# A linear attention's product of keys and values: whole 128x128 blocks against each head's own 32x32 block in four column groups

## The chip, the cores and the metric

The kernel runs on one core of a Trainium2 chip. The metric is the device time of one execution in microseconds (us). The core has a matrix engine (TensorE, PE in the profile, with its weight loads shown apart as PEld), VectorE (DVE), ScalarE (ACT), GpSimd (POOL) and a queue for transfers (SyncE, SP). Each engine works through its own list of instructions in order and waits on semaphores for the others.

## The reference

Two layers, each an attention and a feed-forward part with a layer norm after each. The change touches the attention of the first layer, a linear attention with 16 heads of 32 columns over 2 sequences of 1024 rows of 512 columns:

```
q = _feature_map(proj(Wq))          # elu(y) + 1, heads of 32 columns
k = _feature_map(proj(Wk))
v = proj(Wv)
kv = jnp.einsum('bhtd,bhte->bhde', k, v)
z = 1.0 / (jnp.einsum('bhtd,bhd->bht', q, k.sum(axis=2)) + 1e-06)
out = jnp.einsum('bhtd,bhde,bht->bhte', q, kv, z)
out = out.transpose(0, 2, 1, 3).reshape(b, t, c)
return jnp.einsum('btc,oc->bto', out, Wo)
```

`kv` is one 32x32 block for each head. All inputs are fp32.

## The kernel before

**Tiling.** The 2048 rows are four blocks of 512 (`blk`), two for each sequence (`b`). P is 128 and KC is 4, the number of 128-column tiles in 512 columns. `c` counts such a tile and `j` a head within it, so that column c*128 + 32*j begins one head.

**The order of products.** v is never formed. `add_xk` (L441) sums G = x^T k over a sequence in four PSUM banks (512x512) and copies it to `G_of[b]`. `values` (L501) then multiplies Wv with G. Of that 512x512 product only the 32x32 block of each head is needed. Before the change each 128x128 block on the diagonal is formed, one for each c: four matmuls over k, 128 columns of weights, 128 columns streamed, into one bank `vk` (L508). Each such block holds its four heads' blocks on its own diagonal and twelve others that nobody reads. ScalarE copies the whole bank to `vkm` (L512). `G_rows` (L530) multiplies each head's block with the 32 rows of Wo of that head: sixteen 32x32 matmuls of 512 columns (L538), tile `gp`, in four banks, head j of all tiles in bank `gp[j]`; ScalarE copies them back to `G_of[b]` (L542). The output is q times this G (`o_products`, L560, line L572), added to x.

**What stands around it.** `q_products(j)` is a product by seven multiplications (`by_seven`, L385), given as a generator that yields between its steps; its matmuls are at L396, tiles `grow`, `P2` and `P7` (both shown as `P`). `run` (L660) puts other work between its steps. For the second block j of a sequence the steps are these: the first product (`grow`), then `values(b)`; the second product (`P2`; its sum into the pair is L414 on VectorE), then `turned(i, 0)` and `turned(i, 1)`, two transposes of 128 rows of q of the block before (L239 called from L552, tile `qTp`, copied out by ScalarE at L558); two more products, then `turned(i, 2)`, `turned(i, 3)`, `q_sums` (L521) and `G_rows(b)`; then the products of the output.

The rows that `turned` transposes have been scaled on VectorE by `weigh` (L484): for each 128 rows a product with the sums of k (L491), a sum over each head (L492), an addition (L493), a reciprocal (L494) and a multiplication (L496). In the second sequence, `L414` is queued behind the last of these by hand (`behind_add`), and so is the split of x's transposes (L273). ScalarE's exponentials in `elu1` (L345) are L350 and L351, VectorE's part L352. VectorE also unpacks the feed-forward weights in this time (L293, L294).

**What sets the order.** The matmuls follow each other in the order in which the code is written: `behind()` (L367) ties each group to the last one (`last_pe`). On the other engines a few instructions are tied by `tc.issue_after`; the order of the rest is sorted when the program is built.

**Banks.** `mm_bank` takes two banks by turns, so that vk has the bank that P7 of the product before had (read by L432), P2 of its own product has the other, and P7 of its own product takes vk's bank again. `acc_bank` takes four by turns: the four `qTp`, then the four `gp` in the same banks. So `gp[j]` waits for the copy L558 of `turned(i, j)`.

## Time and profile before

| | us |
|---|---|
| median of 3 runs | 873.0 (872.01 to 873.72) |
| the profiled execution, its own time | 872.3 |
| its span in the profile | 870.5 |
| PE busy | 861.3 (99%), 4067 matmul passes |
| PE weight loads busy | 682.9 (78%) |
| DVE busy | 681.4 (78%) |
| ACT busy | 373.7 (43%) |
| POOL busy | 265.0 (30%) |
| vk, passes (L508) | 64 of 0.275 each, first at 72.7, last at 186.6 |
| vkm, copy (L512) | 2 of 0.586 |
| gp, passes (L538) | 64 of 0.600 each, first at 83.3, last at 195.4 |

The span is what the profile's records cover; the time holds 1.8 us more around it. The 16 matmuls of vk in each batch show as 32 passes, since each fp32 matmul is recorded as two. A pass's duration reaches from its start to its modelled end, and passes overlap, so that what a row of passes costs is read from their starts. Times of single instructions below are from the start of the span; a line of a timeline gives start, length, engine, code line, operation, output<-inputs and shape, and in brackets the idle time ahead of it and what ended that.

### The profile page before, as it was taken

The page shows a single profiled execution, that of the slowest core. Times are in us where ns is not written, and L with a number is a line of the kernel's source. Part 1 is how long each engine was busy: PE and PEld are TensorE (multiplying, and loading weights), DVE is VectorE, ACT ScalarE, POOL GpSimd, SP SyncE. Part 2 cuts the span into 40 slices and gives each one's busy share as a digit, 9 for nine tenths or more (in the row PEclk, how much of TensorE's full clock was granted, in tenths as well). Part 3 has the DMA queues.
Part 4 walks back from the last instruction along what each step waited for, and adds up shares of the span by engine and source line. Part 5 has one row for each costly group of instructions (what it writes and reads, how often), then busy time and mean ns, then how long its engine had stood idle before and what let it go on. Part 6 is the DMA issues. An engine that isn't in the chain of part 4 may idle for free.

```text
span 870.5 us, 11281 instructions
## 1 busy us (share of the span) xinstructions
PE 861.3 (99%) x4067; PEld 682.9 (78%) x4067; DVE 681.4 (78%) x1340; ACT 373.7 (43%) x636; POOL 265.0 (30%) x249
## 2 busy tenths in 40 slices
PE   9999999999999999999999999999999999999996
PEld 6667886678578888888887787888686888888885
DVE  3668984988877788887787988677988988998525
ACT  2345333453468797787886624132210222210000
POOL 2120020830474367457556312030520210000112
PEclk9999999999999999999999999999999999999999
DMA  9632212210241302504301654000154140320001
GB/s 336 225 104 66 82 50 78 73 49 12 68 152 49 49 1 55 91 1 120 75 0 37 133 99 193 1 1 1 38 117 161 50 74 28 118 97 1 25 24 49
DMA packets 103848, 64.87 MB, mean 75 GB/s; under 512 B 80078, under 2 KB 80634, under 8 KB 103281
## 3 DMA queue, kind: packets, MB, share of 16 engines
q1 hardware_dynamic: 101153, 58.89, 24.0%
q0 software_dynamic: 1920, 4.22, 1.3%
q10 hardware_dynamic: 720, 1.05, 0.4%
q8 instruction: 32, 0.52, 0.3%
q14 instruction: 23, 0.19, 0.1%
HBM read 48.37 MB, written 17.88 MB: 76 GB/s over the span
## 4 chain that ended last, share of the span: by engine, by line
PE 88%; issue 4%; POOL 3%; DVE 3%; DMA 1%; POOLq 0%; ACT 0%; DVEq 0%
PE hp L1696 11%; PE yp L1790 11%; PE go L921 10%; PE yp L953 9%; PE gatep L953 9%; PE upp L953 9%; PE grow L396 4%; PE xk L448 4%; PE P L396 3%; PE ao L1561 3%; PE grow L572 2%; POOL x L223 2%; PE kp L646 2%; PE P L572 2%; PE grow L1521 2%
## 5 line engine op out<-in xcount | busy, mean ns | idle before, releaser
L1018 DVE TENSOR_TENSOR yp<-yp,ratio 128x512 f32<-128x512 f32 x160 | 103.2, 693 | 18.2 <-PE yp L953 16.2
L978 ACT ACTIVATE gatep<-gatep,scale 128x512 f32<-128x512 f32 x132 | 84.0, 659 | 36.3 <-PE gatep L953 33.3
L218 POOL TENSOR_TENSOR rs<-rs,table 128x4 f32<-128x4 f32 (+1 forms) x19 | 16.6, 875 | 251.2 <-DVE rs L217 250.9
L953 PE MATMUL yp<-wdn,hhi 128*128 128x512 f32 x176 | 70.3, 399 | 0.2 <-DVE yp L1018 0.2
L953 PE MATMUL gatep<-x1Th,wgu 128*128 128x512 f32 x176 | 70.3, 400 | 0.0
L953 PE MATMUL yp<-wdn,hlo 128*128 128x512 f32 x176 | 69.9, 397 | 0.2 <-POOL hlo L987 0.2
L953 PE MATMUL gatep<-x1Tl,wgu 128*128 128x512 f32 x176 | 69.1, 393 | 0.0
L953 PE MATMUL upp<-x1Tl,wgu 128*128 128x512 f32 x176 | 68.9, 391 | 0.0
L953 PE MATMUL upp<-x1Th,wgu 128*128 128x512 f32 x176 | 68.9, 391 | 0.0
L978 ACT ACTIVATE upp<-upp,scale 128x512 f32<-128x512 f32 x100 | 64.8, 663 | 6.6 <-PE upp L953 3.1
L987 POOL TENSOR_TENSOR hlo<-whole,hhi 128x512 fp32r<-128x512 f32 x43 | 55.5, 1291 | 3.5
L986 POOL CAST hhi<-whole 128x512 fp32r<-128x512 f32 x43 | 26.3, 611 | 86.4 <-DVE whole L984 85.7
L984 DVE SCALAR_TENSOR_TENSOR whole<-upp,scale,silu 128x512 f32<-128x512 f32 x43 | 32.3, 750 | 19.8 <-PE upp L953 12.2
L921 PE MATMUL go<-spare,spare 128*128 128x256 f32 x192 | 44.1, 382 | 0.0
L448 PE MATMUL xk<-pair,x 128*128 128x512 f32 x96 | 42.7, 592 | 0.0
L230 DVE BATCH_NORM_STATS2 st<-x 128x6 f32<-128x512 f32 x64 | 42.3, 676 | 0.3
L953 PEld LDWEIGHTS yp<-wdn,hhi 128*128 128x128 f32 x176 | 33.1, 188 | 10.3 <-DVE yp L1018 1.3
L953 PEld LDWEIGHTS gatep<-x1Th,wgu 128*128 128x128 f32 x176 | 33.1, 188 | 9.1 <-ACT gatep L978 1.1
L921 PEld LDWEIGHTS go<-spare,spare 128*128 128x128 f32 x192 | 36.1, 190 | 5.1
L953 PEld LDWEIGHTS yp<-wdn,hlo 128*128 128x128 f32 x176 | 33.1, 188 | 7.8 <-POOL hlo L987 0.6
L953 PEld LDWEIGHTS gatep<-x1Tl,wgu 128*128 128x128 f32 x176 | 33.1, 188 | 7.5 <-issue 0.2
L953 PEld LDWEIGHTS upp<-x1Th,wgu 128*128 128x128 f32 x176 | 33.1, 188 | 7.3 <-DVE rw L984 0.2
(461 smaller groups left out, 2036.2 us busy)
## 6 DMA issues: line engine op xcount, KB each, us to landing
pk<-in_gu SPq DMA_DIRECT2D x16, 352.0 KB, 3.6
x<-in_x SPq DMA_DIRECT2D x4, 1024.0 KB, 14.1
w<-in_w SPq DMA_DIRECT2D x1, 4096.0 KB, 12.6
w<-in_w SPq DMA_DIRECT2D x4, 1024.0 KB, 5.3
out<-x SPq DMA_DIRECT2D x4, 1024.0 KB, 4.2
x0T<-in_xT SPq DMA_DIRECT2D x3, 1024.0 KB, 7.3
x1r<-x SPq DMA_DIRECT2D x3, 1024.0 KB, 4.3
x1S<-x1r SPq DMA_DIRECT2D x12, 256.0 KB, 4.5
```

The source lines that it names most:

```text
L230: nc.vector.bn_stats(st, x)
L396: ins = nc.tensor.matmul(ps[:, 256 * r : 256 * r + 256], a[:, k, r * P : (r + 1) * P], b[:, k], start=first and r == 0 and k == 0, stop=k ...
L448: ins = nc.tensor.matmul(acc_of[b][c], x_t[blk][:, i, c * P : (c + 1) * P], pairs_of["k", blk][i // 2][:, i % 2], start=blk % 2 == 0 and i ...
L572: ins = nc.tensor.matmul(ps[:, 256 * r : 256 * r + 256], a[:, k, r * P : (r + 1) * P], b[:, k], start=first and r == 0 and k == 0, stop=k ...
L921: ins = nc.tensor.matmul(ps[:, 256 * m : 256 * m + 256], w[:, k, m], b[:, k, 256 * half : 256 * half + 256], start=first and m == 0 and k ...
L953: nc.tensor.matmul(ps, w, x, start=start and n == 0, stop=stop and n == 1, skip_group_check=True)
L978: nc.scalar.activation(ps, ps, AF.Copy, scale=s)
L984: nc.vector.scalar_tensor_tensor(self.whole, ps, s, self.silu, ALU.mult, ALU.mult)
L987: nc.gpsimd.tensor_sub(lo, self.whole, hi.bitcast(F32))
L1018: nc.vector.tensor_tensor(self.y[:, i] if g == NI - 1 else ps, ps, ratio[:, g], ALU.mult)
L1696: ins = nc.tensor.matmul(ps[:, 256 * j : 256 * j + 256], pair_of(w, g)[:, k, j], x[:, k], start=k == 0, stop=k == 1).ins
L1790: nc.tensor.matmul(ps[:, 256 * r : 256 * r + 256], x(r, j), w(j), start=j == 0, stop=j == NJ - 1)
```

## The change

In `values`, each head's block is formed alone. A matmul takes the head's 32 columns of Wv as weights and streams the head's 32 columns of G, both over 128 rows. Head j's result goes to partitions 32*j to 32*j + 31 of the bank, that is to the j-th group of 32 of the array's columns, and to columns 32*c to 32*c + 31. The four heads of a tile follow each other inside the loop over k. There are 64 matmuls per batch where there were 16. `vkm` has 32 columns for each tile instead of 128, ScalarE copies 128 columns of the bank instead of 512, and `G_rows` takes its weights from the narrower tile.

```diff
         with behind():
             for c in range(KC):
-                cut = slice(c * P, (c + 1) * P)
                 for k in range(KC):
-                    ins = nc.tensor.matmul(vk[:, cut], Wv[:, k, cut], G_of[b][:, k, cut], start=k == 0, stop=k == KC - 1).ins
+                    for j in range(4):
+                        head = slice(c * P + 32 * j, c * P + 32 * j + 32)
+                        ins = nc.tensor.matmul(
+                            vk[32 * j : 32 * j + 32, 32 * c : 32 * c + 32], Wv[:, k, head], G_of[b][:, k, head],
+                            start=k == 0, stop=k == KC - 1, skip_group_check=True,
+                        ).ins
         last_pe[0] = ins
-        vkm_of[b] = wk.tile([P, KC, P], F32, tag="vkm", name="vkm", bufs=1)
-
-        nc.scalar.copy(vkm_of[b], vk.rearrange("p (c d) -> p c d", c=KC))
+        vkm_of[b] = wk.tile([P, KC, 32], F32, tag="vkm", name="vkm", bufs=1)
+
+        nc.scalar.copy(vkm_of[b], vk[:, :P].rearrange("p (c d) -> p c d", c=KC))
...
-                        gp[j][quad(c)], vkm_of[b][quad(j), c, quad(j)], Wo[quad(j), c], start=True, stop=True
+                        gp[j][quad(c)], vkm_of[b][quad(j), c], Wo[quad(j), c], start=True, stop=True
```

## The prediction, made before the changed kernel was run

> **What bounds the kernel now.** I read the busy shares in 40 slices first, then the busy time by stages, then the chain of waits, then the timelines around the two places that the change touches.

> ```profile
> PE   9999999999999999999999999999999999999996
> ...
> DVE  3668984988877788887787988677988988998525
> ```

> ```profile
> 70.00:92.00 22.00, 22.00 (x150) 18.57 (x149) 20.19 (x41) 11.98 (x22) 0.00 (x0) 1.00 0.26 81
> 183.00:205.00 22.00, 22.00 (x156) 18.79 (x155) 19.92 (x40) 11.89 (x21) 0.00 (x0) 1.00 0.13 48
> ```

> ```profile
> 72.85 3.62 PE vk L508 x32
> 76.47 1.73 PE P L396 x8
> 78.20 0.87 PE qTp L239 x8
> ```

> The columns of the second view are the stretch, its length, then busy time and count of PE, weight loads, DVE, ACT and POOL, clock, DMA share, GB/s. TensorE (PE) is never idle in the two stretches with `values`, and the chain of waits runs through all of vk: 3.62 us per batch, 7.2 us in all. That alone would promise a gain. But DVE has 20.19 of 22 us of work in the same stretch, so it is a second bound right beside the first.

> **The price of the new block.** vk now takes 3.62 us from its first matmul (72.69) to the next product (76.31): 16 matmuls in 32 passes (the profile shows two for each fp32 matmul), 0.112 us apart. The change has 64 matmuls, so 128 passes and 128 weight loads per batch, each of 32 columns in and 32 out. No row has 128x32 weights with 32 columns streamed. The nearest rows:

> ```profile
> 486.35 0.16 PEld L866 LDWEIGHTS up<-x,rw 128*32 128x32 f32 x8 [0.33 <-issue]
> 486.35 1.07 PE L866 MATMUL up<-x,rw 128*32 128x512 f32 x8
> 492.91 1.17 PE L1389 MATMUL op<-qs,S 32*128 32x128 f32 x32
> 592.36 0.28 PE L1332 MATMUL sc<-kq 32*64 32x64 f32 x4
> 592.46 0.24 PE L1332 MATMUL sc<-kq 32*64 32x64 f32 x4
> 592.52 0.31 PE L1332 MATMUL sc<-qs,km 32*64 32x64 f32 x12
> ```

> L866 has the very weights, in the four column groups: eight loads in 0.16 us, while the first matmuls run. So the groups do work side by side. L1332 has small passes: 24 from 592.36 to 592.83, of which the last takes 0.22, so 24 starts in 0.25 us, 11 ns each. L1389: 32 passes of 128 columns in four groups, the last starting 0.90 us after the first (1.17 less its own 0.27), 28 ns each; a quarter of the columns at a quarter of that is 7 ns. The low end is thus 128 x 7 ns = 0.9 us. The high end has no overlap at all: two passes of one group in L1332 lie 60 ns apart (592.46 to 592.52), 128 x 60 ns = 7.7 us. I take L1332, the smallest passes: 128 x 11 ns = 1.4 us.

> [...]

> Going to another tiling of the array and back has a price that the trace has at gp (32x32 tiles): the product after it starts at 85.12, 0.07 before gp's 83.33 + 1.86 has ended, where P after vk starts 0.16 before vk's end (76.31 against 72.69 + 3.78), and it is busy 1.99 instead of 1.89: 0.2 us on the way out. On the way in gp starts 0.08 before the transposes end and its first passes take 0.612 instead of 0.587: 0.1 us. Together 0.3 us. The block is then 1.4 + 0.3 = 1.7 us (1.2 to 8.0) instead of 3.62: PE is 1.9 us ahead per batch.

> **Where the 1.9 us go, batch 0.** The next product P needs xT, Wq and the other bank of its pair, all long there: it starts at 74.4 and ends at 76.1. Then come the transposes of q, which read what DVE has scaled in L496.

> ```profile
> 75.39 1.29 DVE L496 TENSOR_TENSOR pair<-pair,z 128x512 f32<-128x512 f32 x2
> 79.78 0.68 DVE L414 TENSOR_TENSOR pair<-pair,P 128x512 f32<-128x512 f32 x1
> 81.97 0.68 DVE L496 TENSOR_TENSOR pair<-pair,z 128x512 f32<-128x512 f32 x1
> 82.59 0.26 PEld L239 LDWEIGHTS qTp<-table,pair 128*128 128x128 f32 x2
> ```

> The first two rows are ready at 76.04 and 76.68, so turned(1) starts at 76.73 and PE has lost 0.6 of its lead. Products at 77.2 and 78.9 follow, to 80.6. turned(2) waits for the third L496, 80.66 + 0.69, until 81.40. turned(3) waits for the fourth: it ends at 81.97 + 0.68 = 82.65. The last fenced line holds turned(3)'s first load: it ends at 82.85 and takes 0.14, so it began at 82.71, 0.05 after L496. That 0.05 is the delay with which vk's first load (72.63) follows L432 (71.90 + 0.68). turned(3) is thus held by DVE already, and the whole lead is gone there. DVE can't come earlier: between 72.50 and 82.65 it is busy 10.11 of 10.15 us, and none of it waits for vk.

> What is left is the turn-around: ACT copies turned(2) out (L558) at 82.2 instead of 83.00, so the second copy, which had to queue until 83.53, can start when turned(3) ends at 83.40: at 83.44. gp's last quarter waits for that copy's bank, and starts 0.09 us sooner. Behind the waiting transposes PE has only gp and the products after it in its queue, and those need the same chain. After gp PE is the bound again, and keeps 0.1 us.

> **Batch 1.** PE leads by 1.9 us again, and turned(0..2) lie up to 1.7 us earlier. The end of the chain is on ACT:

> ```profile
> 192.53 0.63 ACT L350 ACTIVATE e<-pair 128x512 f32<-128x512 f32 x1 [0.25 <-DVE pair L414]
> 193.19 0.63 ACT L351 ACTIVATE e<-e 128x512 f32<-128x512 f32 x1
> 193.85 1.07 ACT L558 COPY qT<-qTp 128x512 f32<-128x512 f32 x2
> ```

> L350 waits for DVE's L414 and stands ahead of the copies L558 on ACT, and gp waits for L558's banks. L414 is put behind the last L496 by hand in this batch, and DVE is busy 10.76 of 10.95 us from 182.90 on. The gain is 0.

> **The other edits.** ACT's copy of vk shrinks from 128x512 (0.586 us) to 128x128, about 0.27 between the copies of 128x88 (0.232) and 128x256 (0.378); ACT idles 0.8 us before it, so nothing follows; if that cover went, 0.3 us per batch would be gained. gp's weights keep their 32x32 shape. PE has 2 x 192 instructions more. PE's 8,134 come in the page's 32 instruction packets, so two packets more; PE idles 9.2 us in all (870.5 less 861.3), so a packet costs at most 0.3 us, 0.6 in all; I take 0, as the lead covers it.

> The order of DVE's work is not that of the code (L493, L414, L494, L493, L496 alternate between rows), so something sorts it by estimated times, and vk's new price may sort it anew. In batch 0, if L414 and L421 (0.6 each) leave their places ahead of the last L496, turned(3) comes 1.2 us sooner; if L352 and the two L293/L294 (0.69 + 0.58 + 0.52) move ahead of it, 1.8 later. I take 0 and keep both. In batch 1 L414 and L273 are tied behind L496 by hand.

> **Sum.** The profiled execution took 872.3 us (span 870.5), 0.7 below the median 873.0. 872.3 - 0.1 - 0 = 872.2, so against the median 872.9.

> **Rivals.** *Faster:* the lead survives. For it: PE 99% busy, vk wholly in the chain. Against: the 0.05 us at turned(3). If the sorting frees both places, 2 x 1.9 us: 869.2 (868.2 at the low end of the block); with batch 0's 1.2 alone 871.7, which is no measurable change. *Slower by the passes:* if the column groups don't overlap, or 128 passes can't be fed, the block outgrows 3.62 and PE, which has no slack on this side, loses all of it. It decides from (3.62 - 0.3)/128 = 26 ns a pass, is measurable from 33 ns, and at 60 ns costs 2 x 4.4 us: 881.7. For it: no row shows more than 32 passes in one run, so the feed is untested beyond. Against: L866 and L1332. *Slower by sorting:* DVE work put ahead of L496, 1.8 us: 874.7, and more if later stages are shuffled too.

> **How the numbers follow.** Forecast 0.56: no change that can be measured, that is within 0.2% (1.75 us; what a measurement of this kernel can tell from none), 871.25 to 874.75; its own range 871.5 to 874.5. Faster 0.20. Slower 0.24: 0.12 by the passes, 0.12 by sorting. The time is that of the forecast, 872.9; the range reaches half way into both sides, 869.3 to 876.2, and leaves about 0.08 and 0.10 out.

> **What would show it.** Right: vk takes 1.2 to 2 us; in batch 0 PE's loads idle some 0.8 us ahead of each of turned(2) and turned(3), put down to DVE L496; in batch 1 some 1.7 us within gp, put down to ACT L558; gp's last quarter ends within 0.3 us of where it did, counted from the end of the product ahead of vk. The block's price is wrong if vk's passes lie over 26 ns apart; the forecast is wrong if gp comes over 1 us sooner, or if DVE's order between 72 and 83 us differs.

## The result, and the profile after

The change made the kernel slower by a little: median 873.92 us (871.99 to 876.4, 20 executions) against 872.19 (871.3 to 873.72, 20 executions) of the kernel before, ratio 1.0021 with a 95% interval of 1.0011 to 1.0031.

The median hides two groups. Nine executions have a mean granted TensorE clock of 0.998 or 0.999 and a median of 872.41, which is before's time. Nine have 0.993 or 0.994 and a median of 875.86; two lie between, at 0.996. In 118 executions of the kernel before, run beside the experiments, the clock was never under 0.997 (one of them took 875.57 at 0.998, all others 873.79 or less). So there are two questions: why the block's own gain brought nothing at full clock, and what takes 3.45 us more in the slower group.

The profile shown for the changed kernel is of an execution of the first group (871.99 us, clock 0.998). Its view by tile, for vk and its copy (count, shortest/median/longest ns of one, first and last start, shape):

```profile
L509 PEld LDWEIGHTS vk<-G,Wv x256: 106/109/113, 72.6 to 184.3; 128*32 128x32 f32 x128
L509 PE MATMUL vk<-G,Wv x256: 196/196/217, 72.6 to 184.3; 128*32 128x32 f32 x128
L516 ACT COPY vkm<-vk x2: 247/248/248, 74.7 to 186.0; 128x128 f32<-128x128 f32 x2
```

A pass lasts 0.196 us, yet 128 of them fit into 1.2 us (second fence from here: vk from 72.57, P from 73.79), one start every 10 ns. The passes in the four column groups overlap as hoped. Now the stretches that the prediction showed:

```profile
70.00:92.00 22.00, 20.19 (x244) 15.50 (x243) 19.75 (x40) 11.57 (x21) 0.00 (x0) 1.00 0.25 82
183.00:205.00 22.00, 21.60 (x253) 16.58 (x252) 20.21 (x40) 11.32 (x21) 0.00 (x0) 1.00 0.13 49
```

PE, which was busy for all 22 us of both, now stands still for 1.8 and 0.4 us there. The timeline tells where that is in the first sequence (batch 0):

```profile
72.57 1.30 PE L509 MATMUL vk<-G,Wv 128*32 128x32 f32 x128
73.79 1.99 PE L396 MATMUL P<-Wq,x0T 128*128 128x256 f32 x8
76.97 0.68 DVE L414 TENSOR_TENSOR pair<-pair,P 128x512 f32<-128x512 f32 x1
81.66 0.66 PE L239 MATMUL qTp<-table,pair 128*128 128x128 f32 x4 [1.04 <-DVE pair L496]
81.69 0.63 DVE L352 SCALAR_TENSOR_TENSOR pair<-pair,e 128x512 f32<-128x512 f32 x1
82.23 0.68 DVE L496 TENSOR_TENSOR pair<-pair,z 128x512 f32<-128x512 f32 x1
82.96 0.65 PE L239 MATMUL qTp<-table,pair 128*128 128x128 f32 x4 [0.65 <-DVE pair L496]
```

The groups turned(2) and turned(3) of transposes of q wait 1.04 and 0.65 us for DVE's L496; a third wait, of 0.13 us, lies ahead of turned(0) at 75.91. The chain of waits, which ran through vk before, has turned to DVE there ("issue" is time for which the profile shows no wait):

```profile
81.84 0.39 issue
82.23 0.69 DVE pair L496
82.96 0.65 PE qTp L239 x4
83.62 1.74 PE gp L542 x32
```

In batch 1 the timeline shows ScalarE in the way:

```profile
192.52 0.63 ACT L350 ACTIVATE e<-pair 128x512 f32<-128x512 f32 x1 [1.49 <-DVE pair L414]
192.93 2.81 PE L542 MATMUL gp<-Wo,vkm 32*32 32x512 f32 x32
194.68 0.15 PEld L542 LDWEIGHTS gp<-Wo,vkm 32*32 32x32 f32 x8 [0.85 <-ACT qT L562]
```

L350 waits for DVE, the copies L562 stand behind it, and gp, stretched to 2.81 us, waits for these inside itself. All this concerns the full clock. The rest is a matter of the clock, and of the experiments.

### The profile page after: what moved, and what is told of

Read it like the earlier page. It is cut to its first block, busy times and chain, and to the rows that moved or that the text cites. A ratio compares the mean times of both kernels' runs of the same rounds, so it can differ in the third digit from the quotient of the medians.

```text
span 870.2 us, 11666 instructions
## 1 busy us (share of the span) xinstructions
PE 858.9 (99%) x4259; PEld 676.4 (78%) x4259; DVE 681.0 (78%) x1340; ACT 373.2 (43%) x636; POOL 264.5 (30%) x249
## 2 busy tenths in 40 slices
PE   9999999999999999999999999999999999999996
DVE  3668984988877788887787988677988988998525
## 3 DMA queue, kind: packets, MB, share of 16 engines
q10 hardware_dynamic: 720, 1.05, 0.4%
## 4 chain that ended last, share of the span: by engine, by line
PE 91%; DVE 5%; DMA 1%; issue 1%; POOL 1%; ACT 1%; POOLq 0%; DVEq 0%
PE hp L1700 11%; PE yp L1794 11%; PE go L925 10%; PE yp L957 9%; PE gatep L957 9%; PE upp L957 9%; PE xk L448 6%; PE grow L396 5%; PE P L396 3%; PE ao L1565 3%; PE grow L576 2%; PE P L576 2%; PE kp L650 2%; PE grow L1525 2%; PE op L1373 1%; PE P L1525 1%
```

## The experiments

Each row gives the median and range in us, the executions, and the ratio to the kernel before on the same chip (medians there 872.54 to 872.68) with its 95% interval. "Groups" splits the executions at a mean clock of 0.9965, with the medians of both parts.

| kernel | time (range), n | ratio | groups |
|---|---|---|---|
| e1_again | 876.42 (873.75–877.34), 5 | 1.0048 [1.0035, 1.0061] | 1 at 873.75, 4 at 876.7 |
| e2_fill | 873.04 (871.95–874.03), 11 | 1.0005 [0.9997, 1.0014] | one |
| e3_half | 875.14 (872.26–877.0), 12 | 1.0027 [1.0014, 1.0041] | 5 at 872.6, 7 at 876.7 |
| e4_gp_first | 872.92 (870.25–873.86), 12 | 0.9997 [0.9987, 1.0006] | 6 at 871.4, 6 at 873.3 |
| e5_look | 873.05, 1 | | clock 0.998 |
| e6_batch0 | 875.93 (872.76–876.76), 12 | 1.0032 [1.0022, 1.0042] | 1 at 872.8, 11 at 876.0 |
| e7_batch1 | 872.58 (871.63–874.31), 11 | 1.0001 [0.9992, 1.0010] | 7 at 872.3, 4 at 873.6 |
| e8_gp_fill | 871.92 (871.58–872.55), 11 | 0.9993 [0.9984, 1.0002] | one |
| e9_b1_gp | 870.59 (870.12–871.23), 10 | 0.9978 [0.9969, 0.9988] | one |
| e10_tied | 873.19 (872.87–873.87), 11 | 1.0007 [0.9998, 1.0016] | one |
| e11_less_fill | 875.37 (872.3–875.8), 12 | 1.0022 [1.0013, 1.0031] | see there |
| e12_gp_only | 871.19 (870.76–872.59), 11 | 0.9987 [0.9978, 0.9995] | one |
| e13_late_store | 872.48 (871.8–873.06), 11 | 1.0000 [0.9991, 1.0009] | one |
| e14_b1_gp_late | 871.96 (871.22–872.87), 11 | 0.9994 [0.9985, 1.0003] | one |
| e15_late_store | 874.54 (872.34–876.73), 10 | 1.0019 [1.0008, 1.0029] | 3 at 872.4, 7 at 875.3 |
| e16_look | 876.79, 1 | | clock 0.994 |

**The change again, unaltered (e1_again).**

> The changed kernel once more, unaltered, to see its executions one by one. Clock theory: TensorE now stands still for some 0.3 to 1.4 us at several places (ahead of the transposes of q in batch 0, inside gp in batch 1), and in some executions the granted clock drops for a few us because of that; then the executions fall into two groups, near 872.3 us at a mean clock of 0.998 and near 875.5 us at 0.994, and a profile of the second kind shows the clock at 0.5 for some 7 us at one place near 73 to 90 us or 183 to 200 us. Chain theory: the new order on VectorE and the waits themselves cost 1 to 2 us in every execution alike; then there is one group near 874 us, and the clock is 0.998 in all.

Both groups came back, four of five in the slow one. These executions were on chip 15; e16_look below, on chip 12, is as slow, so the effect is not that of one chip.

**Filling the standstill (e2_fill).** Nine matmuls of ones, into columns of vk's bank that nobody reads, give PE back the time that the block saves. They stand in `values`, behind its loops.

```diff
+            for _ in range(9):
+                ins = nc.tensor.matmul(vk[:, P : 2 * P], ones, ones, start=True, stop=True, skip_group_check=True).ins
         last_pe[0] = ins
```

> The changed kernel with nine more 128x128 matmuls of ones behind vk's 64, into columns of the bank that nobody reads, so that TensorE has as much to do there as before (18 passes of 0.112 us = 2.0 us, with vk's 1.3 + 0.3 us together 3.6). Clock theory: TensorE no longer stands still, all executions near 872.3 us at a clock of 0.998, ratio to the kernel before 0.999 to 1.001. Column theory (the passes of 32 columns themselves lower the clock): still two groups, ratio 1.002 or more. Chain theory: VectorE's order stays the new one, 0.3 to 0.5 us over the kernel before, one group.

One group, at before's time. Work that computes nothing removed the slow group (all eleven at a clock of 0.997 or more): it is not the new block itself that is slow.

**A short block without column groups (e3_half).** The old 128x128 blocks, with half of each sum left out.

```diff
-                for k in range(KC):
-                    ins = nc.tensor.matmul(vk[:, cut], Wv[:, k, cut], G_of[b][:, k, cut], start=k == 0, stop=k == KC - 1).ins
+                for k in range(2):
+                    ins = nc.tensor.matmul(vk[:, cut], Wv[:, k, cut], G_of[b][:, k, cut], start=k == 0, stop=k == 1).ins
```

> The kernel before, whole 128x128 blocks, but with only the first two of the four steps of k summed in vk (half of this sum is left out), so that vk takes 1.8 us instead of 3.6 without any column groups. Clock theory: TensorE gains the same lead, waits for VectorE and ScalarE at the same places, and the executions fall into two groups, 872 and 875 to 876 us, ratio 1.001 to 1.003. Column theory: one group at 0.998, ratio 0.998 to 1.000, as nothing is left that lowers the clock.

Two groups 4 us apart again, with no column group in the kernel. A shorter block is enough; the 32-column form is not needed for it.

**gp ahead of the waiting transposes (e4_gp_first).** In both batches gp no longer stands behind turned(2) and turned(3).

```diff
-            turns(i, 2, 3) + step(q_sums, i) + step(G_rows, b) + split[1],
-            some_o(i, 2) + split[2] + some_o(i, 1) + job(1 - b),
+            step(G_rows, b) + split[1],
+            turns(i, 2, 3) + step(q_sums, i) + some_o(i, 2) + split[2] + some_o(i, 1) + job(1 - b),
```

> The changed kernel with gp put ahead of turned(2) and turned(3), and those one product later, behind the product after gp, where TensorE used to wait: gp needs vkm alone. Clock theory and my reading of the waits: TensorE is filled again, the lead of 1.9 us per batch is kept in part, all executions at 0.998, 868.5 to 871 us, ratio 0.996 to 0.9985. If VectorE is the bound over the whole stretch and not only at the transposes: no gain, ratio 0.999 to 1.001. Chain theory without the clock: a gain, but no difference in how the executions scatter.

The order does bring time in six executions, with a median of 871.4, and two of them lie at 870.3; the median of all misses the 868.5 to 871 that was expected. But a new standstill comes in batch 0, and with it the clock falls. Its timeline, and then its stretches, show both:

```profile
91.65 3.20 PE L576 MATMUL grow<-staged,qS 128*128 128x256 f32 x8 [2.43 <-DVE x L582]
```

```profile
88.87:92.28 3.41, 0.98 (x5) 0.58 (x4) 3.35 (x7) 1.26 (x2) 0.00 (x0) 1.00 0.13 45
92.28:95.70 3.42, 3.42 (x10) 2.71 (x9) 2.53 (x5) 0.00 (x0) 0.00 (x0) 0.50 0.02 5
```

PE waits 2.43 us for DVE, and from 92.28 on, for 3.41 us, the granted clock is 0.50 with PE fully busy: as an estimate, half of it, 1.7 us, is lost.

**The unaltered change, one profiled execution each (e5_look, e16_look).** These were to catch the clock's fall in a profile.

> The changed kernel once more for a profile. Nine of its twenty executions so far, and four of the next five, had a mean clock of 0.993 or 0.994, so the odds are over even that this one is of that kind. Clock theory: then the clock in the records is 0.5 for one or two stretches of 3.41 us each, beginning within 3.4 us after a standstill of TensorE (80 to 84 us, or 187 to 195 us), and passes of 256 columns lie 0.43 us apart there instead of 0.216. Otherwise the time is near 872.5 us and the clock is 1.00 throughout.

> The changed kernel, unaltered, once more for a profile of one of its slow executions, of which the records so far hold none (the change in batch 0 alone gave one: clock 0.5 from 84.3 to 91.1 us). Clock theory: if it is a slow one, 875 us or more at 0.993 or 0.994, the clock is 0.5 for 6.83 us from some point between 82 and 88 us. Fetch theory: if it is slow, the clock is 1.00 there and the time is lost in batch 1.

The first execution fell into the undisturbed group and showed no fall. The second shows it. Its stretches in steps of the clock's records:

```profile
81.99:85.40 3.41, 1.84 (x32) 1.04 (x32) 3.40 (x9) 1.11 (x3) 0.00 (x0) 1.00 0.00 0
85.40:88.81 3.41, 3.41 (x35) 1.37 (x12) 2.28 (x4) 2.65 (x6) 0.00 (x0) 0.50 0.00 0
88.81:92.23 3.42, 3.42 (x9) 2.70 (x8) 1.70 (x3) 0.75 (x2) 0.00 (x0) 0.50 0.38 105
92.23:95.64 3.41, 3.41 (x17) 3.00 (x16) 2.41 (x5) 1.26 (x2) 0.00 (x0) 1.00 0.02 5
```

The clock is 0.50 for two stretches, 6.83 us together, and a product of eight passes takes 3.78 us there (from 87.41), where in the profile shown above it takes 1.99 at full clock. As an estimate, half of 6.83, 3.4 us of work, is lost: about the distance between the two groups (875.86 less 872.41 is 3.45). The fall follows at once on the stretch with the two waits for L496.

**One batch at a time (e6_batch0, e7_batch1).** The change in one sequence only; the other keeps the old block. e6 shown, e7 is its mirror.

```diff
+                cut = slice(c * P, (c + 1) * P)
                 for k in range(KC):
+                    if b != 0:
+                        ins = nc.tensor.matmul(vk[:, cut], Wv[:, k, cut], G_of[b][:, k, cut], start=k == 0, stop=k == KC - 1).ins
+                        continue
                     for j in range(4):
...
+        n = 32 if b == 0 else P
...
```

> The change in batch 0 alone; batch 1 forms whole 128x128 blocks as before. Clock theory: TensorE's two standstills of 1.0 and 0.65 us lie in batch 0, 0.7 us apart, so the two groups stay: some 872.5, some 875 to 876 us, ratio 1.001 to 1.004. If batch 1's waits (0.3 to 1.0 us, and gp's quarters) lower the clock: one group, ratio 0.999 to 1.001.

> The change in batch 1 alone. Clock theory, with the place in batch 0: one group near 872 us at 0.998, ratio 0.998 to 1.000 (batch 1's gp began 0.3 us sooner in the profile of the change). If the place is in batch 1: two groups, ratio 1.001 or more.

Batch 0 carries the loss: 11 of 12 executions at 876.0. Batch 1 alone gives back before's time, but not in the one group that was expected. In its profile, at 872.09, batch 1 takes 31.12 us from vk to the transpose that ends the stage (tile pg, L757 before), against 31.50 before: a gain of 0.4 us. Four of its executions have a clock of 0.996 and are 1.3 us slower than the others; as an estimate from e4, one stretch of 3.41 us at 0.50 costs 1.7 us and lowers the mean clock by 0.002 (1.7 of 870). So batch 1 may lose the clock at times too, for one stretch; no profile caught it there.

**gp first, with batch 0's standstill filled (e8_gp_fill).** As e4, and nine matmuls of ones ahead of the product of batch 0 that waited 2.43 us there.

```diff
+        side = acc_bank("P7")
+        if blk == 0:
+            with behind():
+                for _ in range(9):
+                    last_pe[0] = nc.tensor.matmul(side[:, :P], ones, ones, start=True, stop=True, skip_group_check=True).ins
...
-        side = acc_bank("P7")
```

> The kernel with gp ahead of turned(2), and in batch 0 nine matmuls of ones (18 passes, 2.0 us) into P7's bank, right where TensorE stood still for 2.43 us in that kernel's profile, ahead of the product of q with the second sums. Clock theory: the slower group of that kernel (873 to 873.9 us at 0.995 or 0.996) is gone, all executions 869.8 to 871.5 us at 0.997 or more, ratio 0.997 to 0.999. If the slower group has another cause than the standstill: two groups as there, ratio 0.9985 to 1.001.

One group, 871.92: the fall is gone, but batch 0 gains nothing. From its vk to batch 1's, PE takes 111.24 us instead of the 110.41 before; 0.1 of these 0.8 us have come by the product behind the filling, the rest later on, which no run explains. Batch 1 takes 29.84 us from vk to pg here, 1.7 less than before. Hence the next two kernels.

**The best version (e9_b1_gp, e12_gp_only).** e9: batch 0 as before, batch 1 with the new block and gp ahead of turned(2). e12: only that order, the old block in both. The lines of the order are the same in both; those of e9's block are as in e7.

```diff
-            turns(i, 2, 3) + step(q_sums, i) + step(G_rows, b) + split[1],
-            some_o(i, 2) + split[2] + some_o(i, 1) + job(1 - b),
+            ([] if b else turns(i, 2, 3) + step(q_sums, i)) + step(G_rows, b) + split[1],
+            (turns(i, 2, 3) + step(q_sums, i) if b else []) + some_o(i, 2) + split[2] + some_o(i, 1) + job(1 - b),
```

> Batch 0 as in the kernel before; batch 1 with the change, and there gp ahead of turned(2) and turned(3), which come one product later. From vk of batch 1 to the transpose at the stage's end the kernel before took 31.50 us, the change alone in batch 1 31.12, with gp ahead 29.83: 1.67 us less than before, and batch 0 has no standstill. Clock theory: one group at 0.997 or more near 870.8 us, ratio 0.997 to 0.9987. If a standstill of 0.6 us in batch 1 is enough to lower the clock: two groups, ratio 0.999 to 1.001.

> The kernel before, whole 128x128 blocks in both batches, with only gp put ahead of turned(2) and turned(3) in batch 1. It tells how much of the gain of the kernel with the change in batch 1 and gp ahead comes from the column groups. If TensorE is the bound there, as in the profile of before, the order alone gives at most what gp waited for its banks (0.3 us): ratio 0.9990 to 1.0005. If the order alone frees the chain: 0.998.

e9 is 2.0 us (0.2%) faster than before and beats both kernels. e12 alone brings 1.4 of them, so most of the gain is the order; the 0.6 left for the block is no more than the width of the intervals. The timelines of batch 1 show why, first that of before, then that of e9:

```profile
194.18 1.86 PE L538 MATMUL gp<-Wo,vkm 32*32 32x512 f32 x32
```

```profile
191.48 1.14 PE L547 MATMUL gp<-Wo,vkm 32*32 32x512 f32 x32
193.01 0.66 PE L239 MATMUL x1Tp<-table,x 128*128 128x128 f32 x4 [0.39 <-DVE x1Tl L273]
```

gp takes 1.14 us (in e12 too) in place of 1.86 before and 2.81 in the change, since its banks no longer wait for the copies behind L350.

**DVE's order restored in part (e10_tied).** L414 tied behind the last L496 in batch 0 too.

```diff
-            q_products(j, lambda t: None, weighed[0] if b else None),
+            q_products(j, lambda t: None, weighed[0]),
```

> The changed kernel with L414 tied behind the last L496 in batch 0 too, so that VectorE no longer puts it ahead of the scaling of q. Sorting theory (the new order on VectorE is what costs): the order is mended, one group, ratio 0.999 to 1.0005. Clock theory: the last L496 ends as early as in the kernel before, but TensorE still has 1.9 us less to do and stands still for some 1.6 us in two pieces, so the two groups stay, ratio 1.001 to 1.004.

The expectation of the clock missed: the standstills shrank only to 0.57 and 0.65 us, as the timeline below shows, and yet all executions are in one group, at 873.19.

```profile
81.89 0.66 PE L239 MATMUL qTp<-table,pair 128*128 128x128 f32 x4 [0.57 <-DVE pair L496]
83.19 0.66 PE L239 MATMUL qTp<-table,pair 128*128 128x128 f32 x4 [0.65 <-DVE pair L496]
```

So the kernel with 1.22 us of standstill in its profile kept its clock (0.997 to 0.999) in all eleven executions, where the change, with 1.7 us, did not (0.993 or 0.994 in nine of 20).

**Half of the filling (e11_less_fill).** As e2 with `range(4)`.

> The changed kernel with four matmuls of ones behind vk instead of nine (8 passes, 0.9 us), so that some 0.8 us of standstill is left in batch 0. Clock theory with a threshold in the idle part of a window of 3.41 us (1.63 us idle left the clock alone in one profile, 1.70 and 2.43 us lowered it): one group, ratio 0.999 to 1.001. If any standstill can do it: two groups, the slow one rarer than in the change.

In batch 0 the standstills (0.66 and 0.23 us) left the clock alone. But nine of twelve executions are slow, for a reason that nobody had foreseen: in batch 1 PE stands still in the middle of a product whose operands are all there.

```profile
185.37 0.60 PE L396 MATMUL P<-Wq,x0T 128*128 128x256 f32 x2
188.92 2.37 PE L396 MATMUL P<-Wq,x0T 128*128 128x256 f32 x6 [2.95 <-issue]
```

"issue" means that the profile shows nothing it waits for. Of the transfers, one packet of the page's instruction queue q8 runs only from 186.73 to 187.65, and the write of x1r (1 MB) keeps the transfer engines busy from 183.36 to 186.73. So PE may be waiting for its own instructions, if q8 brings them, which the page doesn't say; it goes on at 188.92, 1.27 us after the packet has landed.

**The write moved away (e13_late_store, e15_late_store, e14_b1_gp_late).** The x1r write of block 1 goes to ScalarE's queue, behind gp's copies: in e11 (e13), in the change (e15) and in e9 (e14). `put_rows` gets the queue as `by`.

```diff
         for c in range(KC):
-            nc.scalar.copy(G_of[b][:, c], gp[c])
+            copied = nc.scalar.copy(G_of[b][:, c], gp[c]).ins
+        if b:
+            with tc.issue_after(copied):
+                put_rows(1, "x1r", by=nc.scalar)
...
-        put_rows(1, "x1r")
```

> The change with four matmuls of ones behind vk, and the 1 MB write of block 1's rows (x1r), which runs from 183 to 187 us, moved to ScalarE's queue behind gp's copies of batch 1 (some 196 us). In the kernel without that move TensorE stood still for 2.95 us in the middle of a product of batch 1, for nothing that the profile shows, while an instruction packet came only after that write had ended; nine of its twelve executions were at 874.8 to 875.8 us. Theory of the instruction fetch (vk's 256 instructions use up a packet in 1.2 us and the next one waits behind the write): the standstill is under 0.5 us, one group near 872.3 us, ratio 0.999 to 1.0005. Otherwise: the two groups stay.

> The change with the same write moved. Clock theory with the place in batch 0 (standstills of 1.04 and 0.65 us there): the two groups stay, some executions near 872 us and some at 875 to 876 us at 0.993 or 0.994, as batch 0 is untouched; the faster group gains up to the 0.3 to 1.0 us that TensorE stood still in batch 1. If the instruction fetch in batch 1 is what makes the change's slow executions: one group near 872 us, ratio 0.999 to 1.0005.

> The fastest kernel so far (the change in batch 1 alone, gp ahead there, 870.6 us) with the same write moved. Its profile had 0.39 us of standstill in batch 1 with an instruction packet coming at 187.1, after the write. Fetch theory: at most that is gained, 870.2 us, ratio 0.997 to 0.998. If the later write delays the next stage's first rows: 870.6 to 872.

In e13 the 2.95 us become 0.48, and all eleven executions lie at 871.8 to 873.06:

```profile
187.49 1.46 PE L396 MATMUL P<-Wq,x0T 128*128 128x256 f32 x6 [0.48 <-issue]
```

That fits a wait for instructions in e11: the packet now runs from 185.14 to 186.06, and PE goes on 1.43 us after that. The standstills marked "issue" in batch 1 of the change itself end in the same way, 1.25 to 1.30 us after a packet has landed (at 187.04 in the profile shown, 188.62 in e1_again, 188.32 in e5_look). In e15 the two groups stay, and its profile (876.73 us) has the clock at 0.50 from 85.13 for 6.83 us: so in the change itself the slower group goes back to batch 0 and not to that write. In e14 the expected gain did not come: PE has new standstills of 0.95 us from 200.7 and 0.52 from 216.8, both ended by DVE, and the kernel is 1.4 us slower than e9. Why DVE is later there the runs don't tell.

**When the granted clock fell, read from all profiles.** Each trace records when the granted clock changes. In one execution the changes lie whole multiples of 3.413 us apart: 863.57 us, 253 of them, in the profiles of before and of the change, 3.41 in e4, 6.83 in e16. They lie elsewhere in each execution (the first record of full clock begins 4.41 us into the span in before, 3.90 in the change). So the work of PE in each such window can be added up, transposes and products apart (us):

```
kernel          window           products  transposes  clock in the next
e4_gp_first      88.87 -  92.29    0.99       0.00       0.50
e16_look         81.99 -  85.40    0.60       1.24       0.50
e15_late_store   81.71 -  85.13    0.48       1.24       0.50
e6_batch0        80.88 -  84.29    0.48       1.24       0.50
e11_less_fill   185.89 - 189.31    0.47       0.00       0.50
e10_tied        186.68 - 190.10    0.80       1.47       1.00
e10_tied         80.87 -  84.28    0.95       1.24       1.00
e3_half          79.56 -  82.97    1.12       0.66       1.00
e11_less_fill   865.15 - 868.56    1.45       0.00       1.00
after            78.99 -  82.40    1.63       0.66       1.00
```

Idle time alone doesn't sort these: e3_half's window holds less busy time in all (1.78) than e16's (1.84), e11's at the end only 1.45, and both keep the clock. Products alone don't either: e10's 0.80 keeps it, e4's 0.99 doesn't. An estimate from the ten windows: with a transpose counted at 0.3 of its time, the five ahead of a fall come to 0.47 to 0.99 us and the five others to 1.24 to 1.83; weights from 0.15 to 0.6 sort them too. The profiles of before and of the change have one more fall each, at the kernel's end, behind a window in which PE does nothing (864.57 to 867.98 and 864.05 to 867.47, with a clock of 0.50 from there on); their other whole windows come to 1.83 or more at that weight. So the estimate rests mainly on the five falls above. It was made afterwards from the profiles, and no run was made to test it.

The estimate also suggests why the execution matters. In the changed kernel's batch 0 no product runs from 80.62, where the one before ends, to gp at 83.55: 2.93 us, two transposes and two standstills. A window that covers all of it holds 0.48 us of products; where the windows split it, each side holds more:

```profile
78.99:82.40 3.41, 2.28 (x12) 1.51 (x10) 3.40 (x10) 1.80 (x4) 0.00 (x0) 1.00 0.00 0
82.40:85.82 3.42, 2.86 (x38) 1.26 (x39) 3.33 (x6) 2.27 (x4) 0.00 (x0) 1.00 0.00 0
```

These are the two windows of the undisturbed profile of the change: 2.28 and 2.86 us busy, clock 1.00 throughout. How often it happens is not explained by this alone: of all places where the windows could start, 24% (for the bound of 0.99) to 42% (for 1.24) give such a window in batch 0, in the profile of the change as in that of e6, and yet eleven of twelve executions of e6 were slow. The kernel before has PE busy all through this place; its lowest window, short of the kernel's end, holds 2.39 us of products. In e6 two standstills of 1.05 and 0.65 us, with transposes between them, came ahead of the fall: the clock is 0.50 from 84.29 on.

## Why the prediction was right or wrong

- **The block, 1.7 us with the switching: right in kind, 0.4 us too long.** vk to the next product takes 1.22 us, and that product is busy 1.99 instead of 1.89, as forecast for the way out of the other tiling: 1.3 us in all, so that PE was 2.3 us ahead and not 1.9. Passes start 10 ns apart (1.2 us over 128), next to the 11 taken from L1332. The rival *slower by the passes* is out.
- **The lead lost at L496 in batch 0: right in place, a little worse in size.** 1.04 and 0.65 us of standstill were found where 0.8 and 0.8 were forecast. gp starts 0.22 us later than before (0.34 counted from vk's first pass) instead of 0.1 sooner. "PE has lost 0.6 of its lead" at turned(1) does not fit the prediction's own times: its 77.2 for the next product against 78.91 before leaves 1.7 of 1.9.
- **The order of DVE's work: taken as unchanged, wrong by 0.3 to 0.5 us.** In batch 0 L414 moved ahead of the two L491, L421 ahead of both L494 and L352 ahead of the last L496, so that this starts at 82.23 instead of 81.97, 0.26 us later, or 0.47 counted from L432 ahead of it (71.69 instead of 71.90). That is the rival *slower by sorting*, at about a quarter of its price of 1.8 us. With L414 back behind the last L496, in e10, the first standstill is 0.47 us shorter.
- **Batch 1, gain 0: right within 0.4 us.** gp waits 0.56 and 0.85 us inside itself for the copies L562, as forecast from L350, though at 1.4 us and not 1.7. Between its transposes PE also stands still for 0.29 us with nothing shown to wait for (0.96 in e1_again, 1.02 in e5_look).
- **Two more instruction packets, 0: wrong in kind.** There is one more (33 instead of 32). The cost, forecast as at most 0.3 us each, is not fixed: the standstill that ended behind a packet was 0.29 us in one profile of the change, 0.96 and 1.02 in two others, and 2.95 in e11, where the packet came behind a large write.
- **The sum, 872.2 in the profiled execution: right at full clock.** The nine executions of the first group have a median of 872.41, against 872.19 before. In part two misses cancel there: from batch 0's vk to batch 1's the change takes 110.63 us instead of 110.41, and from there to pg 31.11 instead of 31.50.
- **The step that failed** is "*turned(3) is thus held by DVE already, and the whole lead is gone there*": the prediction let the lead turn into standstill and priced that as time that PE had won and gave back, nothing more. It put nothing for the granted clock, which in e16 was 0.50 for 6.83 us behind that standstill. Nine of 20 executions took a further 3.4 us, and the median of all, 873.92, lies 1.5 us above that of the first group. The rivals had no such case. The forecast was no change, and the kernel became slower; that the median lies in the prediction's own range of 871.5 to 874.5 is luck, since it falls between two groups. e2 (standstill filled, loss gone), e3 (other block, same loss), e6 (batch 0 alone, same loss) and e16 (the fall itself) show it together.

## What to carry to other kernels

Where work is taken from an engine that the next engine can't follow, ask not only where the lead goes but what a standstill there does: here 1.7 us of rest beside transposes cost 3.4 us more in many executions, and with matmuls that compute nothing in its place (e2, 873.04) the median was lower than with rest (e1_again, 876.42). Look for the change of order that lets the freed engine do something else in that time, which here was worth more (1.4 us) than the smaller product itself. And look at single executions: a median between two groups describes neither.
